# Layer 1 of a two-layer attention kernel: division by the softmax sums taken out of the groups, last blocks of two sets turned together, projection run in the drain

## The chip, the cores and the metric

The kernel runs on one core of one Trainium2 chip. The metric is the device time of one execution in microseconds; the median of several executions is compared. The program is unrolled: every loop below is written out into the instruction streams of the engines. TensorE (PE) multiplies and transposes into PSUM (eight banks of 128 partitions x 512 float32), VectorE (DVE), ScalarE (ACT) and GpSimd (POOL) work on elements, and SyncE (SP) issues the DMAs. Each engine takes its instructions in the order in which the program emits them and waits on semaphores for the others.

## The reference

Two layers over N = 4096 nodes with 512 features and 8 heads of 64, all in float32. Layer 0 is a graph attention layer with additive scores; layer 1, cut to what matters here, is

```python
h = jnp.maximum(_layernorm(x), 0.0)
keys, queries, values = (jnp.einsum('nj,hjk->hnk', h, W) for W in (Wks, Wqs, Wvs))
atts = jnp.einsum('hqk,hmk->hqm', queries, keys) / 64 ** 0.5
atts = atts - 1e16 * (1.0 - adj)[None, :, :]          # adj: [4096, 4096]
atts = jax.nn.softmax(atts, axis=-1)
x = x + jnp.einsum('hqm,hmk,hko->qo', atts, values, Wo)
```

## The kernel before

Layer 0 (lines 80 to 488), its last head pair together with the keys, queries and values of layer 1 (to line 780), then layer 1's attention (lines 791 to 1060) and at last the projection by `Wo` (lines 1063 to 1084). The change lies in the last two.

Layer 1 works on a pair of heads `c` (`HC` = 4 of them), then on groups of 128 query rows (`NG` = 32), then on sets of 32 rows (`GS` = 4 a group): 4 x 32 x 4 = 512 sets, one a slot `s` of the main loop (line 1021). A set holds 32 queries on 32 partitions for each of `NS` = 4 blocks of 1024 keys (`QK_`), so that one tile of 128 x 1024 holds 32 whole rows of scores of one head. The ring `t` keeps 12 sets (`RING`), each with two heads.

The order of the work is written by hand: a set passes through the slots with fixed delays. In slot `s`:

- `squares` (line 934, set s-4): DVE transposes 32 x 32 squares in place for columns 0 to 767 of both heads.
- `turned` (line 938, set s-4): PE transposes the last 256 columns (two 128 x 128 blocks for each of two heads) into one PSUM bank, tile `tr`; `taken` (line 947) copies them back to `t` on ACT.
- `smallest` (line 910, odd slots, sets s-3 and s-2): PE gathers the extremes of the four key blocks (`nmB`, a matmul with `bands`), DVE reduces them to `nm`.
- one step of `finish` (line 966) of the last group, see below.
- `scores` (line 871, set s): 32 matmuls of PE into four banks `sc`; `masked` (line 887): four DVE instructions add the penalty `a` and keep the extreme of the row.
- `taken`, then `exps` (line 924, set s-3): ACT takes the exponential in place and adds up the row (`G.sm`).
- `made_penalty` (line 862) for set s+1 where c = 0: Relu on ACT, then POOL makes the penalty from the adjacency; it is stored in `pen_d` and loaded from there for c > 0.
- `parted` (line 900, odd slots): POOL lays out the extremes for `smallest`.
- `weighted` (line 950, set s-8): 32 matmuls of PE with the values, accumulated over the group's four slots in one bank `o`.
- the loads for slot s+5 on SP.

`finish` divides and turns back. It copies `o` to `oT` on ACT, forms the rows' sums by eight-fold short matmuls with `band` (`den`, line 972), takes the reciprocal on DVE (`rden`); one slot later PE transposes `oT` back to rows (`back`, line 979), DVE multiplies (`att`, line 981), and SP stores 128 x 128 to `att_d`, which lies in rows of nodes. PSUM is full: four banks for `sc`, one for `tr`, two for `ms` (`nmB`, `den`, `back`), one for `o`.

After the loop the projection loads, for each of 32 row blocks, 128 rows of `x1_d` and of `att_d`, transposes the latter (`atr`, line 1075), copies it (`aT`), multiplies by `wot` (`oo`, line 1080), adds and stores.

Of the kernel before, what the change touches and what calls it, by code (L numbers as in the profile page):

```python
# [8 lines left out]
F32 = mybir.dt.float32  # L9
# [3 lines left out]
PSUM = bass.MemoryType.PSUM  # L13
DRAM = bass.MemoryType.DRAM

P = 128
# [7 lines left out]
def kernel(  # L24
# [14 lines left out]
    nc = tc.nc  # L39
    N, DM = x.shape  # L40
    H, D = src_proj.shape[1:]
    HD = H * D
    NB = N // P
    KC = DM // P
    HC = HD // P
# [6 lines left out]
    dram = ctx.enter_context(tc.tile_pool(name="dram", bufs=1, space=DRAM))  # L52

    ident = const.tile([P, P], F32, name="ident")
# [5 lines left out]
    SQ = 32  # L60
    NS = P // SQ
    band = const.tile([P, SQ], F32, name="band")
    nc.vector.tensor_reduce(band, ident.rearrange("p (a j) -> p j a", j=SQ), AX.X, ALU.add)
    bands = const.tile([P, P], F32, name="bands")
# [28 lines left out]
    PR = 2 * D  # L93
# [5 lines left out]
    with tc.tile_pool(name="a0k", bufs=1) as pk, tc.tile_pool(name="a0v", bufs=4) as pv, tc.tile_pool(  # L99
        name="a0a", bufs=3  # L100
# [72 lines left out]
        def turned(G, i):  # L173

            trs = []
            for b in range(MB):
                if b % 4 == 0:
                    tr = ptr.tile([P, TW], F32, name="tr")
                    trs.append(tr)
                for h in range(2):  # L180
                    nc.tensor.transpose(  # L181
                        tr[:, bass.ts(b % 4 * 2 + h, P)], G.t[h][:, bass.ts(i * MB + b, P)], ident
                    )
            return trs
# [231 lines left out]
        def step(n):  # L416
            return groups[n // 2], n % 2
# [83 lines left out]
    with tc.tile_pool(name="b0c", bufs=1) as pc, tc.tile_pool(name="b0a", bufs=4) as pa, tc.tile_pool(  # L501
# [114 lines left out]
        def squares(G, k):  # L616
            u = t[:, G.ring + k].rearrange("p h (n j) -> p h n j", j=SQ)
            nc.vector.transpose(u, u)  # L618
# [160 lines left out]
            while jobs:  # L779
                work()  # L780
    l0.close()
    att_d = dram.tile([N, HD], F32, name="att_d")
    pen_d = dram.tile([N // 32, P, N // 4], F32, name="pen_d")

# [5 lines left out]
    VC = 768  # L792
    NV = VC // SQ
    NT = (QK_ - VC) // P
    with tc.tile_pool(name="a1t", bufs=1) as pt, tc.tile_pool(name="a1k", bufs=4) as pkk, tc.tile_pool(
        name="a1v", bufs=GS
    ) as pv, tc.tile_pool(name="a1a", bufs=6) as pa, tc.tile_pool(name="a1q", bufs=2) as pq, tc.tile_pool(
        name="a1x", bufs=1
    ) as px, tc.tile_pool(name="a1s", bufs=6) as psb, tc.tile_pool(
        name="a1sc", bufs=4, space=PSUM  # L800
    ) as psc, tc.tile_pool(name="a1tr", bufs=1, space=PSUM) as ptr, tc.tile_pool(
        name="a1m", bufs=2, space=PSUM
    ) as pm, tc.tile_pool(name="a1o", bufs=1, space=PSUM) as po:
        t = pt.tile([P, RING, 2, QK_], F32, name="t")
        class Group:


# [115 lines left out]

        def exps(G, k):
            if k == 0:
                G.sm = psb.tile([P, GS, 2], F32, name="sm")
            for h in range(2):
                u = t[:, G.ring + k, h, :]
                nc.scalar.activation(  # L929
                    u, u, AF.Exp, bias=G.nm[k // 2][:, k % 2, h : h + 1], scale=-1.0,  # L930
                    accum_out=G.sm[:, k, h : h + 1],
                )

        def squares(G, k):
# [1 line left out]
            nc.vector.transpose(u, u)  # L936

        def turned(G, k):
            tr = ptr.tile([P, 512], F32, name="tr")
            for h in range(2):  # L940
                for m in range(NT):
                    nc.tensor.transpose(  # L942
                        tr[:, bass.ts(h * NT + m, P)], t[:, G.ring + k, h, bass.ds(VC + m * P, P)], ident
                    )
            return tr

        def taken(G, k, tr):
            nc.scalar.copy(t[:, G.ring + k, :, VC:], tr.rearrange("p (h x) -> p h x", h=2))  # L948

        def weighted(G, i):  # L950
            if i == 0:
# [12 lines left out]
                    )  # L964

        def finish(G):

            oT = px.tile([P, P], F32, name="oT")
            nc.scalar.copy(oT, G.o[:, :P])  # L969
            den = pm.tile([P, 512], F32, tag="ms", name="den")  # L970
            for k in range(GS):
                nc.tensor.matmul(  # L972
                    den[bass.ts(k, SQ), :2], lhsT=band, rhs=G.sm[:, k, :], start=True, stop=True
                )
            rden = psb.tile([P, 2], F32, name="rden")
            nc.vector.reciprocal(rden, den[:, :2])
            yield
            back = pm.tile([P, 512], F32, tag="ms", name="back")
            nc.tensor.transpose(back[:, :P], oT, ident)  # L979
            att = px.tile([P, 2, D], F32, name="att")  # L980
            nc.vector.tensor_mul(
                att, back[:, :P].rearrange("p (h d) -> p h d", d=D),
                rden.unsqueeze(2).to_broadcast([P, 2, D]),
            )
            nc.sync.dma_start(
                att_d[bass.ts(G.g, P), bass.ts(G.c, PR)], att.rearrange("p h d -> p (h d)")
            )

        groups = [Group(c, g) for c in range(HC) for g in range(NG)]
        total = len(groups) * GS  # L990
# [12 lines left out]
        with tc.manual_schedule():  # L1003
            pens = {}

            def prefetch(n):
                if n < total:
                    if n % (QG * GS) == 0:
                        load_queries(n // (QG * GS))
                    pens[n] = penalty(*step(n))  # L1010

            AHEAD = 5
            ending = iter(())
            load_keys(0)
            for n in range(AHEAD):
                prefetch(n)
            with_self(*step(0), pens[0])
            made_penalty(*step(0), pens[0])
            for i in range(GS):
                load_values(0, i)  # L1020
            for s in range(total + PROD + 3):
                if s + 1 < total:
                    with_self(*step(s + 1), pens[s + 1])
                if s < total:
                    keep_penalty(*step(s), pens[s])

                c, at = divmod(s + 4, SETS)
                if 0 < c < HC and at == 0:
                    load_keys(c)
                c, at = divmod(s - PROD - 1 + GS, SETS)  # L1030
                if 0 < c < HC and at < GS:
                    load_values(c, at)
                turn = 0 <= s - TURN < total
                if turn:
                    squares(*step(s - TURN))
                    tr = turned(*step(s - TURN))

                if s % 2 and 0 <= s - 3 < total:
                    G, k = step(s - 3)
                    smallest(G, k // 2)  # L1040
                next(ending, None)
                if s < total:
                    scs = scores(*step(s))
                    masked(*step(s), scs, pens.pop(s))
                if turn:
                    taken(*step(s - TURN), tr)
                if 0 <= s - EXPS < total:
                    exps(*step(s - EXPS))
                if s + 1 < total:
                    made_penalty(*step(s + 1), pens[s + 1])  # L1050
                if s % 2 and s < total:
                    G, k = step(s)
                    parted(G, k // 2)
                n = s - PROD
                if 0 <= n < total:
                    W, w = step(n)
                    weighted(W, w)
                    if w == GS - 1:
                        ending = finish(W)
                prefetch(s + AHEAD)  # L1060


    with tc.tile_pool(name="p3c", bufs=1) as pc, tc.tile_pool(name="p3", bufs=4) as pw, tc.tile_pool(
        name="p3t", bufs=3, space=PSUM
    ) as pst, tc.tile_pool(name="p3m", bufs=3, space=PSUM) as psm:
        wot = pc.tile([P, HC, DM], F32, name="wot")
        nc.scalar.dma_start(wot, wo.rearrange("h d o -> (h d) o").rearrange("(c p) o -> p c o", p=P))
        for rb in range(NB):
            xt = pw.tile([P, DM], F32, name="xt")
            nc.sync.dma_start(xt, x1_d[bass.ts(rb, P), :])  # L1070
            at = pw.tile([P, HD], F32, name="at")
            nc.sync.dma_start(at, att_d[bass.ts(rb, P), :])
            tr = pst.tile([P, 512], F32, name="atr")
            for c in range(HC):
                nc.tensor.transpose(tr[:, bass.ts(c, P)], at[:, bass.ts(c, P)], ident)
            aT = pw.tile([P, HD], F32, name="aT")
            nc.scalar.copy(aT, tr)  # L1077
            o = psm.tile([P, 512], F32, name="oo")
            for c in range(HC):
                nc.tensor.matmul(  # L1080
                    o, lhsT=aT[:, bass.ts(c, P)], rhs=wot[:, c, :], start=(c == 0), stop=(c == HC - 1)
                )
            nc.vector.tensor_add(xt, xt, o)
            nc.sync.dma_start(out[bass.ts(rb, P), :], xt)


# [26 lines left out]
```

## Time and profile before

| what | value |
|---|---|
| time, median of 3 runs | 5032.46 us (5031.23 to 5033.24) |
| profiled execution: its time, its span | 5033.3 us, 5031.5 us |
| PE, DVE, ACT, POOL busy, of the span | 95%, 90%, 78%, 7% |
| granted TensorE clock, mean | 0.978 |
| layer 1: first and last start of `sc` | 2542.8 and 4862.8 us |
| projection: first `atr`, last `oo` | 4893.6 and 5027.1 us |
| one `o` group of 32 matmuls, `sc` of 32, four `tr` | 1.97, 1.95, 0.66 us |

Times are from the start of the span. A PE matmul's duration reaches over the beginning of the next, so what an operation takes of PE is read from the starts of what follows. PEld is PE's loading of weights, which overlaps matmuls. In the listings a row gives the start, the duration, the engine, the line, the operation, the tiles written and read, and in brackets the engine's idle time before it with what ended it. "issue" is time in which the engine waited for nothing that the profile shows.

### The profile page before, as it was taken

What the parts mean: (1) busy time and instruction counts of PE and PEld (TensorE: products, weight loads), DVE (VectorE), ACT (ScalarE), POOL (GpSimd) and SP (SyncE); (2) the same over time, 40 slices, a digit from 0 to 9 for tenths busy, and PEclk for the clock granted to TensorE, in tenths of its full rate; (3) what the DMA queues carried; (4) which work ended last, traced back from release to release, by engine and by line L of the source; (5) the groups of instructions that cost most, each with busy time, mean ns of one, the idle gap of its engine ahead of it and who ended that gap; (6) DMA issues with size and microseconds to landing.
All of it is one profiled execution on the core that took longest, in us unless ns stands there. A gap on an engine that the chain in (4) does not pass through costs nothing.

```text
span 5031.5 us, 147684 instructions
## 1 busy us (share of the span) xinstructions
PE 4802.4 (95%) x62810; PEld 3552.2 (71%) x62810; DVE 4530.7 (90%) x8205; ACT 3929.0 (78%) x4581; POOL 362.1 (7%) x648
## 2 busy tenths in 40 slices
PE   6999999999999869999989999999999999999999
PEld 5888888888888757677746666666666666666654
DVE  4999999999999898888579999999999999999971
ACT  3999999999999898888568888666666666666651
POOL 1000000000000011111112222000000000000000
PEclk8999999999999979999999999999999999999999
DMA  6444454445444474444387777433353434444425
GB/s 217 152 163 146 163 194 163 147 161 195 163 147 161 129 167 134 141 140 138 98 240 240 237 239 246 145 124 126 126 160 122 127 127 143 141 127 127 127 98 176
DMA packets 339908, 794.35 MB, mean 158 GB/s; under 512 B 57520, under 2 KB 168368, under 8 KB 314160
## 3 DMA queue, kind: packets, MB, share of 16 engines
q1 hardware_dynamic: 338720, 783.86, 48.7%
q8 instruction: 493, 8.08, 0.7%
q14 instruction: 167, 1.37, 0.1%
q10 hardware_dynamic: 528, 1.05, 0.1%
HBM read 652.48 MB, written 132.25 MB: 156 GB/s over the span
## 4 chain that ended last, share of the span: by engine, by line
PE 46%; DMA 1%; ACT 1%; issue 1%; DVE 1%; SPq 0%; POOL 0%; ACTq 0%; DVEq 0%; POOLq 0%
PE o L959 18%; PE sc L878 18%; PE tr L942 6%; PE oo L1080 2%; DMA a<-in_adj_dram 1%; ACT t L929 1%; PE nmB L913 1%; PE den L972 0%; DVE t L936 0%; PE back L979 0%; SPq L852 0%; PE mp L697 0%; DVE t L894 0%; ACT aT L1077 0%; PE mpv L709 0%
## 5 line engine op out<-in xcount | busy, mean ns | idle before, releaser
L894 DVE CUSTOM_DVE_ANT_0 t<-sc,a 128x512 f32<-128x512 f32 x2048 | 1291.1, 686 | 78.2 <-issue 56.3
L929 ACT ACTIVATE t<-t,nm 128x1024 f32<-128x1024 f32 x1024 | 1168.4, 1143 | 167.6 <-DVE nm L918 167.6
L959 PEld LDWEIGHTS o<-t,v 128*64 128x64 f32 x16384 | 883.9, 137 | 423.2 <-issue 339.7
L878 PE MATMUL sc<-k,q 64*32 64x512 f32 x16384 | 1002.5, 597 | 8.9 <-DVE nm L894 8.9
L959 PE MATMUL o<-t,v 128*64 128x128 f32 x16384 | 1007.0, 276 | 0.2 <-ACT oT L969 0.2
L936 DVE STREAM_TRANSPOSE t<-t 128x1536 f32<-128x1536 f32 x512 | 908.1, 1774 | 8.9 <-ACT t L929 5.9
L158 DVE CUSTOM_DVE_ANT_0 t<-t,a 128x2048 f32<-128x2048 f32 x384 | 876.1, 2282 | 28.7 <-ACT t L147 23.6
L181 PE MATMUL tr<-ident,t 128*128 128x128 f32 x6144 | 781.7, 278 | 38.1 <-ACT pT L190 20.0
L181 PEld LDWEIGHTS tr<-ident,t 128*128 128x128 f32 x6144 | 665.4, 141 | 130.6 <-issue 65.5
L203 PE MATMUL o<-pT,v 128*64 128x128 f32 x12288 | 756.8, 276 | 0.8 <-DVE pT L192 0.8
L147 ACT ACTIVATE t<-tb,src 128x4096 f32<-128x4096 f32 x192 | 732.0, 3813 | 13.7 <-DMA tb<-trg_d 13.7
L168 ACT ACTIVATE t<-t,nm 128x4096 f32<-128x4096 f32 x192 | 731.7, 3811 | 6.9 <-DVE nm L163 6.6
L203 PEld LDWEIGHTS o<-pT,v 128*64 128x64 f32 x12288 | 664.1, 137 | 60.7 <-issue 46.9
L948 ACT COPY t<-tr 128x512 f32<-128x512 f32 x512 | 298.9, 584 | 480.2 <-PE tr L942 477.4
L192 DVE COPY pT<-tr 128x1024 f32<-128x1024 f32 x549 | 652.7, 1214 | 9.8 <-PE tr L181 9.8
L878 PEld LDWEIGHTS sc<-k,q 64*32 64x32 f32 x16384 | 251.0, 106 | 340.7 <-issue 298.5
L942 PE MATMUL tr<-ident,t 128*128 128x128 f32 x2048 | 342.6, 287 | 11.5 <-ACT t L929 9.5
L569 ACT ACTIVATE lk<-tb,srcb 128x1024 f32<-128x1024 f32 x256 | 282.3, 1113 | 83.5 <-DVE nm L579 76.4
L579 DVE CUSTOM_DVE_ANT_0 bt<-lk,ba 128x1024 f32<-128x1024 f32 x256 | 301.9, 1215 | 25.6 <-ACT e L703 12.7
L618 DVE STREAM_TRANSPOSE bt<-bt 128x2048 f32<-128x2048 f32 x128 | 295.1, 2306 | 29.0 <-ACT bt L611 29.0
L942 PEld LDWEIGHTS tr<-ident,t 128*128 128x128 f32 x2048 | 213.7, 140 | 111.3 <-issue 85.0
L611 ACT ACTIVATE bt<-bt,nm 128x1024 f32<-128x1024 f32 x256 | 290.3, 1135 | 0.4 <-DVE nm L600 0.3
(116 smaller groups left out, 3961.4 us busy)
## 6 DMA issues: line engine op xcount, KB each, us to landing
a<-in_adj_dram SPq DMA_DIRECT2D x192, 1024.0 KB
a<-pen_d SPq DMA_DIRECT2D x384, 512.0 KB
ba<-in_adj_dram SPq DMA_DIRECT2D x512, 128.0 KB
a<-in_adj_dram SPq DMA_DIRECT2D x512, 128.0 KB
pen_d<-a SPq DMA_DIRECT2D x128, 512.0 KB
h<-hT_d SPq DMA_DIRECT2D x96, 256.0 KB
qk_d<-e SPq DMA_DIRECT2D x64, 256.0 KB
x<-in_x_dram SPq DMA_DIRECT2D x8, 1024.0 KB
```

Source lines behind the costliest of these rows:

```text
L147: nc.scalar.activation(t, targets[G.c, h], AF.Prelu, bias=src[:, G.g, 2 * G.c + h : 2 * G.c + h + 1], alpha=SLOPE)
L158: nc.vector.tensor_tensor_reduce(out=t, in0=t, in1=rows_of_adj[G, f], scale=-1.0, scalar=FMAX, op0=ALU.add, op1=ALU.min, accum_out=nm[:, f ...
L168: nc.scalar.activation(G.t[h], G.t[h], AF.Exp, bias=G.nm[h][:, NCH : NCH + 1], scale=-1.0, accum_out=G.sm[:, h : h + 1],)
L181: nc.tensor.transpose(tr[:, bass.ts(b % 4 * 2 + h, P)], G.t[h][:, bass.ts(i * MB + b, P)], ident)
L192: nc.vector.tensor_copy(pT, tr)
L203: nc.tensor.matmul(G.o[h * D : (h + 1) * D, :P], lhsT=feats[G.c][i][:, b, bass.ts(h, D)], rhs=pT[:, bass.ts(b % 4 * 2 + h, P)], start=(mb ...
L878: nc.tensor.matmul(sc[h][bass.ts(a, SQ), :], lhsT=G.q[bass.ts(h, D), bass.ds(G.q0 + k * SQ, SQ)], rhs=keys[G.c][half][bass.ts(h, D), a, :] ...
L894: nc.vector.tensor_tensor_reduce(out=t[:, G.ring + k, h, cols], in0=scs[half][h], in1=a[:, cols], scale=1.0, scalar=FMAX, op0=ALU.add, op1 ...
L929: nc.scalar.activation(u, u, AF.Exp, bias=G.nm[k // 2][:, k % 2, h : h + 1], scale=-1.0, accum_out=G.sm[:, k, h : h + 1],)
L936: nc.vector.transpose(u, u)
L942: nc.tensor.transpose(tr[:, bass.ts(h * NT + m, P)], t[:, G.ring + k, h, bass.ds(VC + m * P, P)], ident)
L959: nc.tensor.matmul(G.o[bass.ts(h, D), :P], lhsT=v[:, b, bass.ts(h, D)], rhs=t[:, bass.ds(G.ring, GS), h, bass.ds(at, SQ)], start=(mb == 0) ...
```

## The change

- `finish` is one ACT copy of `o` to `oT` and one store, into an `att_d` that now lies as [head pair, 128 features, nodes]. It is emitted at the start of the slot after the group's last `weighted`.
- The sums of all rows are kept in a tile `sums`. Sixteen groups (a half of a head pair) are divided at once: `inverted` forms the sums by one matmul with `bands`, takes the reciprocal, turns it and stores it in `inv_d`; `scaled` loads four pieces of `att_d` of 512 columns with the reciprocals broadcast over the partitions, multiplies on POOL (on DVE for the last half) and stores them back. One step of this is taken in each slot.
- `turned` and `taken` run in odd slots alone, for the sets s-5 and s-4 together: eight transposes into two banks, one copy of 128 x 1024. The pool of `ms` falls from two banks to one.
- The projection needs no transposes, since `att_d` lies turned. Its loads come in chunks of two row blocks; `projected` runs from slot 513 on, one row block a slot, and the rest after the loop. Before the ninth chunk's load all that is left of the last division is emitted.

```diff
@@ -779,8 +779,12 @@
             while jobs:
                 work()
     l0.close()
-    att_d = dram.tile([N, HD], F32, name="att_d")
+    att_d = dram.tile([HC, P, N], F32, name="att_d")
+    inv_d = dram.tile([HC, 2, N], F32, name="inv_d")
     pen_d = dram.tile([N // 32, P, N // 4], F32, name="pen_d")
@@ -792,16 +796,19 @@
     VC = 768
     NV = VC // SQ
     NT = (QK_ - VC) // P
+    SG = NG // 2
     with tc.tile_pool(name="a1t", bufs=1) as pt, tc.tile_pool(name="a1k", bufs=4) as pkk, tc.tile_pool(
         name="a1v", bufs=GS
     ) as pv, tc.tile_pool(name="a1a", bufs=6) as pa, tc.tile_pool(name="a1q", bufs=2) as pq, tc.tile_pool(
-        name="a1x", bufs=1
-    ) as px, tc.tile_pool(name="a1s", bufs=6) as psb, tc.tile_pool(
+        name="a1x", bufs=2
+    ) as px, tc.tile_pool(name="a1s", bufs=6) as psb, tc.tile_pool(name="a1z", bufs=2) as pz, tc.tile_pool(name="a1at", bufs=3) as pat, tc.tile_pool(
         name="a1sc", bufs=4, space=PSUM
     ) as psc, tc.tile_pool(name="a1tr", bufs=1, space=PSUM) as ptr, tc.tile_pool(
-        name="a1m", bufs=2, space=PSUM
+        name="a1m", bufs=1, space=PSUM
     ) as pm, tc.tile_pool(name="a1o", bufs=1, space=PSUM) as po:
         t = pt.tile([P, RING, 2, QK_], F32, name="t")
+        sums = pt.tile([P, HC, 2, 2, SG, GS], F32, name="sums")
         class Group:
@@ -923,12 +930,12 @@
         def exps(G, k):
             if k == 0:
-                G.sm = psb.tile([P, GS, 2], F32, name="sm")
+                G.sm = sums[:, G.c, G.g // SG, :, G.g % SG, :]
             for h in range(2):
                 u = t[:, G.ring + k, h, :]
                 nc.scalar.activation(
                     u, u, AF.Exp, bias=G.nm[k // 2][:, k % 2, h : h + 1], scale=-1.0,
-                    accum_out=G.sm[:, k, h : h + 1],
+                    accum_out=G.sm[:, h, k : k + 1],
                 )
         def squares(G, k):
@@ -936,16 +943,19 @@
             nc.vector.transpose(u, u)
         def turned(G, k):
-            tr = ptr.tile([P, 512], F32, name="tr")
-            for h in range(2):
-                for m in range(NT):
-                    nc.tensor.transpose(
-                        tr[:, bass.ts(h * NT + m, P)], t[:, G.ring + k, h, bass.ds(VC + m * P, P)], ident
-                    )
+            tr = ptr.tile([P, 2, 2, NT * P], F32, name="tr")
+            for j in range(2):
+                for h in range(2):
+                    for m in range(NT):
+                        nc.tensor.transpose(
+                            tr[:, j, h, bass.ts(m, P)],
+                            t[:, G.ring + k - 1 + j, h, bass.ds(VC + m * P, P)], ident,
+                        )
             return tr
         def taken(G, k, tr):
-            nc.scalar.copy(t[:, G.ring + k, :, VC:], tr.rearrange("p (h x) -> p h x", h=2))
+            nc.scalar.copy(t[:, bass.ds(G.ring + k - 1, 2), :, VC:], tr)
         def weighted(G, i):
             if i == 0:
@@ -964,27 +974,88 @@
                     )
         def finish(G):
             oT = px.tile([P, P], F32, name="oT")
             nc.scalar.copy(oT, G.o[:, :P])
-            den = pm.tile([P, 512], F32, tag="ms", name="den")
-            for k in range(GS):
+            nc.sync.dma_start(att_d[G.c, :, bass.ts(G.g, P)], oT)
+        def inverted(c, half):
+            tot = pm.tile([P, 512], F32, tag="ms", name="tot")
+            nc.tensor.matmul(
+                tot[:, : 2 * SG * GS], lhsT=bands,
+                rhs=sums[:, c, half].rearrange("p h g k -> p (h g k)"), start=True, stop=True,
+            )
+            inv = px.tile([P, P], F32, tag="oT", name="inv")
+            nc.vector.reciprocal(inv[:SQ], tot[:SQ, : 2 * SG * GS])
+            yield
+            invT = pm.tile([P, 512], F32, tag="ms", name="invT")
+            nc.tensor.transpose(invT[:, :SQ], inv[:SQ], ident[:SQ, :SQ])
+            rows = px.tile([P, SQ], F32, name="rows")
+            nc.scalar.copy(rows, invT[:, :SQ])
+            for h in range(2):
+                nc.sync.dma_start(
+                    inv_d[c, h, bass.ts(half, SG * P)].rearrange("(q i) -> q i", i=SQ), rows[bass.ts(h, D)]
+                )
+            yield
+        def scaled(c, half):
+            last = (c, half) == (HC - 1, 1)
+            zs = []
+            for i in range(4):
+                cols = bass.ts(half * 4 + i, 4 * P)
+                z = pz.tile([P, 2, 4 * P], F32, tag="z", name="z")
+                nc.sync.dma_start(z[:, 0], att_d[c, :, cols])
+                for h in range(2):
+                    nc.sync.dma_start(z[bass.ts(h, D), 1], inv_d[c, h, cols].partition_broadcast(D))
+                yield
+                zs.append((cols, z))
+                if i % 2 == 0:
+                    continue
+                yield
+                for cols, z in zs:
+                    (nc.vector if last else nc.gpsimd).tensor_mul(z[:, 0], z[:, 0], z[:, 1])
+                yield
+                for cols, z in zs:
+                    nc.sync.dma_start(att_d[c, :, cols], z[:, 0])
+                zs = []
+        def divided(c, half):
+            yield from inverted(c, half)
+            yield from scaled(c, half)
+        ZR = 2
+        chunks = []
+        def load_chunk():
+            i = len(chunks)
+            if i >= NG // 2 // ZR:
+                for d in divisions:
+                    for _ in d:
+                        pass
+                divisions.clear()
+            if i < NB // ZR:
+                at = pat.tile([P, HC, ZR * P], F32, name="at")
+                nc.sync.dma_start(at, att_d[:, :, bass.ts(i, ZR * P)].rearrange("c p n -> p c n"))
+                xt = pa.tile([P, ZR, DM], F32, tag="a", name="xt")
+                nc.sync.dma_start(xt, x1_d[bass.ts(i, ZR * P), :].rearrange("(r p) d -> p r d", p=P))
+                chunks.append((at, xt))
+        def projected(j):
+            if j >= NB:
+                return
+            i, r = divmod(j, ZR)
+            at, xt = chunks[i]
+            o = psc.tile([P, HF], F32, tag="sc", name="oo")
+            for c in range(HC):
                 nc.tensor.matmul(
-                    den[bass.ts(k, SQ), :2], lhsT=band, rhs=G.sm[:, k, :], start=True, stop=True
-                )
-            rden = psb.tile([P, 2], F32, name="rden")
-            nc.vector.reciprocal(rden, den[:, :2])
-            yield
-            back = pm.tile([P, 512], F32, tag="ms", name="back")
-            nc.tensor.transpose(back[:, :P], oT, ident)
-            att = px.tile([P, 2, D], F32, name="att")
-            nc.vector.tensor_mul(
-                att, back[:, :P].rearrange("p (h d) -> p h d", d=D),
-                rden.unsqueeze(2).to_broadcast([P, 2, D]),
-            )
-            nc.sync.dma_start(
-                att_d[bass.ts(G.g, P), bass.ts(G.c, PR)], att.rearrange("p h d -> p (h d)")
-            )
+                    o, lhsT=at[:, c, bass.ts(r, P)], rhs=wot[:, c, :], start=(c == 0), stop=(c == HC - 1)
+                )
+            nc.vector.tensor_add(xt[:, r], xt[:, r], o)
+            if r == ZR - 1:
+                nc.sync.dma_start(out[bass.ts(i, ZR * P), :].rearrange("(r p) d -> p r d", p=P), xt)
+                load_chunk()
         groups = [Group(c, g) for c in range(HC) for g in range(NG)]
         total = len(groups) * GS
@@ -1010,7 +1081,8 @@
                     pens[n] = penalty(*step(n))
             AHEAD = 5
-            ending = iter(())
+            rb = 0
+            divisions = []
             load_keys(0)
             for n in range(AHEAD):
                 prefetch(n)
@@ -1033,12 +1105,19 @@
                 turn = 0 <= s - TURN < total
                 if turn:
                     squares(*step(s - TURN))
+                turn = turn and (s - TURN) % 2
+                if turn:
                     tr = turned(*step(s - TURN))
                 if s % 2 and 0 <= s - 3 < total:
                     G, k = step(s - 3)
                     smallest(G, k // 2)
-                next(ending, None)
+                n = s - PROD
+                if 0 < n <= total and n % GS == 0:
+                    finish(groups[n // GS - 1])
+                if s > total:
+                    projected(rb)
+                    rb += 1
                 if s < total:
                     scs = scores(*step(s))
                     masked(*step(s), scs, pens.pop(s))
@@ -1051,37 +1130,23 @@
                 if s % 2 and s < total:
                     G, k = step(s)
                     parted(G, k // 2)
-                n = s - PROD
                 if 0 <= n < total:
                     W, w = step(n)
                     weighted(W, w)
-                    if w == GS - 1:
-                        ending = finish(W)
+                if n > 1 and n % (SG * GS) == 1:
+                    divisions.append(divided(*divmod(n // (SG * GS) - 1, 2)))
+                for d in divisions[:1]:
+                    if next(d, d) is d:
+                        divisions.pop(0)
+                if s == (HC - 1) * SETS + SETS // 2:
+                    wot = pkk.tile([P, HC, DM], F32, tag="k", name="wot")
+                    nc.sync.dma_start(wot, wo.rearrange("h d o -> (h d) o").rearrange("(c p) o -> p c o", p=P))
+                if s > total - AHEAD and len(chunks) < 3:
+                    load_chunk()
                 prefetch(s + AHEAD)
-    with tc.tile_pool(name="p3c", bufs=1) as pc, tc.tile_pool(name="p3", bufs=4) as pw, tc.tile_pool(
-        name="p3t", bufs=3, space=PSUM
-    ) as pst, tc.tile_pool(name="p3m", bufs=3, space=PSUM) as psm:
-        wot = pc.tile([P, HC, DM], F32, name="wot")
-        nc.scalar.dma_start(wot, wo.rearrange("h d o -> (h d) o").rearrange("(c p) o -> p c o", p=P))
-        for rb in range(NB):
-            xt = pw.tile([P, DM], F32, name="xt")
-            nc.sync.dma_start(xt, x1_d[bass.ts(rb, P), :])
-            at = pw.tile([P, HD], F32, name="at")
-            nc.sync.dma_start(at, att_d[bass.ts(rb, P), :])
-            tr = pst.tile([P, 512], F32, name="atr")
-            for c in range(HC):
-                nc.tensor.transpose(tr[:, bass.ts(c, P)], at[:, bass.ts(c, P)], ident)
-            aT = pw.tile([P, HD], F32, name="aT")
-            nc.scalar.copy(aT, tr)
-            o = psm.tile([P, 512], F32, name="oo")
-            for c in range(HC):
-                nc.tensor.matmul(
-                    o, lhsT=aT[:, bass.ts(c, P)], rhs=wot[:, c, :], start=(c == 0), stop=(c == HC - 1)
-                )
-            nc.vector.tensor_add(xt, xt, o)
-            nc.sync.dma_start(out[bass.ts(rb, P), :], xt)
+            for j in range(rb, NB):
+                projected(j)
 # ---- launch: one core; inputs and outputs as the reference has them ----
```

## The prediction

> **What bounds the kernel now.** I read the page, then the busy times by stage, then the order of time inside a few slots, then the waits, then the chain. The stages first (columns: stretch, length, busy time of PE, PEld, DVE, ACT, POOL, granted clock, DMA share, GB/s): layer 1's first head pair, its last one, the final projection.
>
> ```profile
> core 0: us, PE busy (x) PEld busy (x) DVE busy (x) ACT busy (x) POOL busy (x), PEclk, DMA share, GB/s
> 2560.00:3100.00 540.00, 525.94 (x8169) 321.75 (x8155) 525.36 (x1280) 447.76 (x729) 134.65 (x176) 0.99 0.77 244
> 4300.00:4850.00 550.00, 550.00 (x8692) 344.00 (x8688) 526.91 (x1219) 362.68 (x642) 14.59 (x61) 1.00 0.41 128
> 4900.00:5020.00 120.00, 118.98 (x360) 57.98 (x359) 20.30 (x30) 16.11 (x30) 0.00 (x0) 1.00 0.57 184
> ```
>
> In three of four head pairs PE never stops; DVE idles 23 of 550 us. In the first pair (where the penalty is made) PE idles 14 us too. The projection is PE alone. So PE's order of time in the last pair, four slots less a little (start, us, what):
>
> ```profile
> 4301.87 1.95 PE L878 MATMUL sc<-k,q 64*32 64x512 f32 x32
> 4303.75 1.97 PE L959 MATMUL o<-t,v 128*64 128x128 f32 x32
> 4305.65 0.66 PE L942 MATMUL tr<-ident,t 128*128 128x128 f32 x4
> 4306.23 0.24 PE L972 MATMUL den<-sm,band 128*32 128x2 f32 x8
> 4306.41 1.95 PE L878 MATMUL sc<-k,q 64*32 64x512 f32 x32
> 4308.29 1.97 PE L959 MATMUL o<-t,v 128*64 128x128 f32 x32
> 4310.19 0.66 PE L942 MATMUL tr<-ident,t 128*128 128x128 f32 x4
> 4310.68 0.31 PE L913 MATMUL nmB<-parts,bands 128*128 128x32 f32 x2
> 4310.82 0.31 PE L979 MATMUL back<-ident,oT 128*128 128x128 f32 x1
> 4311.06 1.95 PE L878 MATMUL sc<-k,q 64*32 64x512 f32 x32
> 4312.94 1.97 PE L959 MATMUL o<-t,v 128*64 128x128 f32 x32
> 4314.83 0.66 PE L942 MATMUL tr<-ident,t 128*128 128x128 f32 x4
> 4315.42 1.95 PE L878 MATMUL sc<-k,q 64*32 64x512 f32 x32
> ```
>
> Durations overlap, so costs are differences of starts: sc 1.88, o 1.90 (32 weight loads take 1.73, the rest is a gap of 0.17 before tr). A slot from sc to sc is 4.54 with den, 4.65 with nmB and back, 4.36 with neither, and 4.50 with nmB alone (4315.42 to 4319.93): 18.05 a group of four.
>
> The first pair has another loop. There the mask of an even slot comes right after the penalty that POOL made for it:
>
> ```profile
> 2812.72 1.04 POOL L865 TENSOR_SCALAR a<-a 128x1024 f32<-128x1024 f32 x1 [4.25 <-ACT a L864]
> ...
> 2813.87 0.65 DVE L894 CUSTOM_DVE_ANT_0 t<-sc,a 128x512 f32<-128x512 f32 x1
> ```
>
> And the tail, from the chain: PE falls idle 6.14 us until the attention rows come back, then takes 8.08 us per two row blocks, of which 6.9 are the 16 projection matmuls (0.43 each) and the rest transposes.
>
> ```profile
> 4887.35 6.14 DMA at<-att_d
> ...
> 4902.80 7.13 PE oo L1080 x16
> ```
>
> **The change part by part.** The steady part is c=1 to 3: 96 groups.
>
> Den and back leave PE: 4.54-4.36 = 0.18 and 4.65-4.50 = 0.15, so 0.33 a group. On DVE rden (0.13) and att (0.20 between starts) leave too; there they free an engine that is not the bound.
>
> Turning by twos. An even slot loses tr and the gap after it, 0.59 (4314.83 to 4315.42). An odd slot gets eight transposes for four: layer 0 issues 16 in 1.73, so four more cost 0.43. The unknown is o followed directly by sc, which the trace never shows. Its tiles go from 128*64 to 64*32, and every change of tile shape that it does show (o to tr, tr to sc, tr to den) carries a 0.17 gap in the weight loads. The Trainium skill, "TensorEngine Tiling (Array Packing)", Key Properties, says that a change of tiling mode drains the engine. That speaks against the step: only one drain of the two goes. Bounds: 0 (the pair saves 0.33, the sum falls by 33 more) to 0.34, rows and columns both changing (it saves nothing). I take 0.17, the nearest row, which is inside o's 1.90. A pair of slots goes from 8.86 to 2x(1.88+1.90) + 0.72 + 0.44 = 8.72 (0.72: tr with nmB to sc now, 4319.20 to 4319.93). The group: 18.05 - 0.33 - 2x0.14 = 17.44; times 96, -58.6 us.
>
> Does anything else bind before 8.72? The slots become uneven (PE 3.78 and 4.94), so I laid out one pair from sc of the even slot at 0: o 1.88, tr 3.78, nmB 4.71, sc 4.94, o 6.82. DVE: four masks are 2.45, the 32x32 turning 1.70, nm 0.07 more; 8.37 a pair, so it waits 0.35 for the odd sc (mask 1.27 after sc, as in 4306.41 to 4307.68). ACT: the merged copy starts 1.17 after tr, at 4.95, and by layer 0's copy of the same 128x1024 takes 1.10, to 6.05; nm is ready at 5.97, so exps run 6.05 to 8.43 and the turning on DVE, due at 8.66, is served with 0.2 to spare. The next exps end at 10.8 (11.6 behind an oT copy), the next eight transposes need them at 12.5. ACT's loop through nm, exps, turning, mask, turning is 8.52. PE stays the bound, by 0.2. The copy oT now opens an even slot and ends by 0.4, its o bank is wanted at 1.88. One bank less for ms costs nothing: its reader nm is done two slots before.
>
> First pair, c=0: the loop nm, two exps, Relu, POOL's penalty, mask is 4.67 (2799.98 to 2804.65 in order of time), mask back to nm 4.45 (2813.87 to 2818.32): 9.12 a pair of slots, and the stage runs at just that. Nothing of it is touched; DVE alone would give 0.33 a group, 10 us. I take -1, between 0 and -10.
>
> Divisions, eight halves, seven inside the loop. PE: tot and invT, each like back (0.15 to 0.31) plus a drain: 0.5. DVE: a reciprocal of 128 columns (att's 0.28 is the nearest row) that waits for tot about 0.5; half is in DVE's slack. ACT: rows, 0.2. +4 in all, between 1 and 10. POOL: 28 products of 128x512; from 0.24 us at 32 columns (parts) and 0.46 at 128 (L241), 1.3 each as an estimate, up to 2.1 (L676's 128x512). Two stand ahead of parts, which nmB wants 4.8 us after its masks, and ahead of the next penalty in c=0, which has 4 us: hidden. "SBUF — State Buffer", Terms, has a lock between DVE and GpSimd under which the loser fully blocks: by it 28x1.3 = 36 us of DVE waiting, of which perhaps 20 would show. The trace speaks otherwise for these operations: in c=0, POOL lies under the turning in every slot, and that takes 1775 ns against 1773 later. I take 0. SP: att_d writes stay 128 (behind oT instead of att), and a half adds 12 loads, 6 writes, about 0.35 to 0.45 of issue each. SP stands at the z stores until POOL is done, with the penalty loads behind it; those are five slots (22 us) ahead. Cover enough; if gone, each us late is a us of PE. The extra 24 MB meet a DMA share of 0.41.
>
> The tail, from the last sc (4861.42) to the end, is 170.1 now. After: sc 1.9, nine o 17.1, a wait for exps 1.0, two turns 2.4, 32 projections of 8x0.43 = 110.1, tot and invT 0.9: 133.4. Ten projections fill the draining slots; the aT transposes and copies are gone. But the last half can be divided only after o's last group: the flush after projection 11 runs add 0.7, six issues 2.6, landing 3, two products 1.4, store 2.9, again six issues, landing and products 7, stores 0.8, chunk load 6 (the 6.14 above as top): some 24.5 us, while PE has four projections, 13.8. A stall of 11, then a cold clock (the first eight projection matmuls took 6.29 against 3.7 after the idle 6 us, granted clock 0.52): 2.6. With 3.8 for the last add and store: 151. That is -19, between -33 (no stall) and 0 (30 us of stall).
>
> Sum: -58.6 - 1 + 4 - 19 = -74.6. The profiled execution took 5033.3 (span 5031.5 and 1.8 around it), 0.8 over the median: 4958.7, and against the median 4958.
>
> **The rivals.** (1) o to sc drains twice, or the uneven slots cost what the pairing saves: 0.28x96 = 27 back, 4985. For it: rows and columns of the tile change at once. Against: tr to den also went at 0.17. (2) No drain: pair 8.55, just above ACT's 8.52: 4925. Against: every shape change shown has its gap. (3) The flush stalls PE for 30 us, as each step waits for the whole of att_d: 4977. For it: SP is in order and the loads and stores alternate. (4) Slower: the z loads land late, POOL waits at the product with parts behind it, and nmB, sc and all else stand. The loads have two slots, then parts another two, some 20 us; each us beyond costs one, in 14 rounds (seven halves of two). It eats 74 us and turns the sign from 25 us of landing on. Against: loads land within 6 us in the chain, with DMA at full load. (5) The change does what it says but its gain in c=0 is DVE's 10: 4949.
>
> **How the numbers follow.** My forecast 0.55 (4945 to 4972), (1) 0.14, (2) 0.11, (3) 0.10, (4) with other losses 0.05, (5) 0.05. The range 4926 to 4994 leaves out (4), half of (2) and a combination of (1) with (3). 0.2% (10 us) is what a measurement of this kernel tells from no change. Faster 0.93, same 0.02, slower 0.05.
>
> **What would show it.** Stretches in c=1 to 3: PE busy throughout, 17.4 us a group, odd slots 4.9, even 3.8; the weight loads of sc with a 0.17 gap after o. The copy of tr 256 times at 1.10. DVE idle 0.3 to 0.4 a pair before the odd mask. c=0 unchanged at 9.1 a pair. In the tail an idle PE of about 11 us near projection 16, then 3.44 a row block. The forecast is wrong if PE idles in c=1 to 3 before tr (ACT late) or before nmB (POOL late), or if sc starts over 0.2 after o's last load.

## The result and the profile after

The changed kernel takes 4986.92 us (median of 4 runs, 4984.33 to 4987.83) against 5032.85 us before: ratio 0.9907, 95% interval 0.9889 to 0.9924. It is faster by 46 us; 74.6 were forecast. The profiled execution took 4984.33 us with a span of 4982.5.

Where the time went is read from the starts of the first mask (`masked`) of slots 0, 128 and 511, in the profiled execution of each kernel:

| stage | before | after | difference | forecast |
|---|---|---|---|---|
| up to slot 0 (code not changed) | 2544.1 | 2538.9 | -5.1 | 0 |
| first head pair, c=0 | 590.3 | 622.7 | +32.4 | -1 |
| c=1 to 3, to slot 511 | 1728.3 | 1672.1 | -56.2 | -54.6 (with the divisions) |
| slot 511 to the end | 168.9 | 148.8 | -20.1 | -19 |

The first row is drift: in the other profiles below it lies anywhere from 2539.9 to 2547.8. Two stages came out as worked out; the first head pair went the other way. The busy times by stage (the columns as before) give no hint of it, except that PE is busier in c=0, although the stage is longer:

```profile
2560.00:3100.00 540.00, 532.42 (x7549) 313.30 (x7551) 526.88 (x1169) 418.79 (x634) 132.61 (x170) 0.99 0.74 237
4300.00:4820.00 520.00, 520.00 (x8236) 331.19 (x8228) 502.62 (x1134) 339.96 (x569) 24.34 (x68) 1.00 0.44 147
4850.00:4970.00 120.00, 110.54 (x409) 53.08 (x406) 23.20 (x33) 1.73 (x4) 0.00 (x0) 0.96 0.61 203
```

Before, PE was busy 525.94 of 540 us in the same stretch of c=0 with 8169 matmuls; now 532.42 with 7549. A busy time that rises while the work falls is matmuls that wait inside their own duration. Here they are those of `sc`: 3552 of them take 268.4 us, where 3728 took 229.2, and PE's idle time before them is ended by DVE's masks (9.1 us, 6.0 before), which free their banks.

PE's order of time in the last head pair after, from sc of an even slot on:

```profile
4303.41 1.95 PE L885 MATMUL sc<-k,q 64*32 64x512 f32 x32
4305.29 1.97 PE L969 MATMUL o<-t,v 128*64 128x128 f32 x32
4307.19 1.09 PE L951 MATMUL tr<-ident,t 128*128 128x128 f32 x8
4308.12 0.31 PE L920 MATMUL nmB<-parts,bands 128*128 128x32 f32 x2
4308.35 1.95 PE L885 MATMUL sc<-k,q 64*32 64x512 f32 x32
4310.23 1.97 PE L969 MATMUL o<-t,v 128*64 128x128 f32 x32
4312.13 1.95 PE L885 MATMUL sc<-k,q 64*32 64x512 f32 x32
```

An odd and an even slot last 8.72 (4303.41 to 4312.13), and o followed by sc takes 1.90 (4310.23 to 4312.13).

Now the first head pair, where a pair of slots grew from 9.2 to 9.7. Before, in a slot with `nmB`, DVE's maximum for the self-edges (`with_self`, line 860) was over just before POOL made the penalty (line 865):

```profile
2807.21 0.18 DVE L860 TENSOR_TENSOR a<-a,ident 32x32 f32<-32x32 f32 x1
...
2807.43 1.05 POOL L865 TENSOR_SCALAR a<-a 128x1024 f32<-128x1024 f32 x1 [2.61 <-ACT a L864]
```

In other slots it was closer still. In 22 of the 128 the maximum started ahead of POOL by 0.013 us or less, as here:

```profile
2724.72 0.18 DVE L860 TENSOR_TENSOR a<-a,ident 32x32 f32<-32x32 f32 x1
2724.73 1.08 POOL L865 TENSOR_SCALAR a<-a 128x1024 f32<-128x1024 f32 x1 [2.45 <-ACT a L864]
```

After, POOL is first, and the same maximum (now line 867) takes 0.81:

```profile
2912.87 1.04 POOL L872 TENSOR_SCALAR a<-a 128x1024 f32<-128x1024 f32 x1 [2.12 <-ACT a L871]
2913.03 0.08 DVE L901 DVE_READ_ACCUMULATOR2_ANT nm<- 128x1 f32 x1
2913.14 0.81 DVE L867 TENSOR_TENSOR a<-a,ident 32x32 f32<-32x32 f32 x1
2913.98 1.78 DVE L943 STREAM_TRANSPOSE t<-t 128x1536 f32<-128x1536 f32 x1
```

It ends at 2913.95, 0.04 after POOL does (2913.91). The turning, the next nm and both masks are late by 0.6. In the instruction list 59 of the 128 maxima are so, all but one of every second one from the ninth on. All 128 together take 56.7 us, and 24.2 before. The 32.5 us more are the 32.4 of the table. Nobody is listed as waiting: the time is inside the instruction, so the waits of DVE say nothing. Only the duration of the one instruction does (count, then min/median/max in ns, before and after):

```profile
L860 DVE TENSOR_TENSOR a<-a,ident x128: 169/183/1016, 2536.8 to 3123.9; 32x32 f32<-32x32 f32 x128
```

```profile
L867 DVE TENSOR_TENSOR a<-a,ident x128: 170/189/926, 2531.6 to 3151.2; 32x32 f32<-32x32 f32 x128
```

Even this row hides it: the median still falls on the short half. The one long case before (1.016) was the same collision: there POOL had started 0.06 us ahead of the maximum.

In the tail PE stops once more, for the ninth chunk, as the chain shows:

```profile
4914.97 5.34 DMA at<-att_d
4920.31 0.14 issue
4920.45 57.56 PE oo L1052 x128
```

PE has been idle for 9.46 us when projection 16 starts, and the last 128 matmuls take 57.56 instead of 55.0 (0.43 each); the granted clock was 0.56 from 4920 to 4926 and 1.00 after.

### The profile page after: what moved, and what is told of

It reads as the page before. It is cut to its first block, busy times and chain, and to the rows that moved or that the text cites. A ratio compares the mean times of both kernels' runs of the same rounds, so it can differ in the third digit from the quotient of the medians.

```text
span 4982.5 us, 144240 instructions
## 1 busy us (share of the span) xinstructions
PE 4757.9 (95%) x61554; PEld 3525.6 (71%) x61554; DVE 4522.0 (91%) x7961; ACT 3856.4 (77%) x4301; POOL 396.4 (8%) x676
## 5 line engine op out<-in xcount | busy, mean ns | idle before, releaser
L885 PE MATMUL sc<-k,q 64*32 64x512 f32 x16384 | 1059.3, 598 | 11.9 <-DVE nm L901 11.8
L943 DVE STREAM_TRANSPOSE t<-t 128x1536 f32<-128x1536 f32 x512 | 907.6, 1773 | 4.1 <-ACT t L936 1.1
L181 PE MATMUL tr<-ident,t 128*128 128x128 f32 x6144 | 781.6, 278 | 38.2 <-ACT pT L190 20.1
L181 PEld LDWEIGHTS tr<-ident,t 128*128 128x128 f32 x6144 | 665.3, 141 | 130.7 <-issue 65.4
L958 ACT COPY t<-tr 128x1024 f32<-128x1024 f32 x256 | 259.0, 1012 | 515.1 <-PE tr L951 503.8
L885 PEld LDWEIGHTS sc<-k,q 64*32 64x32 f32 x16384 | 263.2, 106 | 402.0 <-issue 234.1
L626 PE MATMUL bo<-bt,bv 128*64 128x128 f32 x4096 | 284.2, 298 | 6.2 <-ACT boT L635 4.9
L951 PE MATMUL tr<-ident,t 128*128 128x128 f32 x2048 | 280.6, 280 | 2.0 <-ACT t L936 2.0
```

The costliest lines, as they stand in the source:

```text
L181: nc.tensor.transpose(tr[:, bass.ts(b % 4 * 2 + h, P)], G.t[h][:, bass.ts(i * MB + b, P)], ident)
L885: nc.tensor.matmul(sc[h][bass.ts(a, SQ), :], lhsT=G.q[bass.ts(h, D), bass.ds(G.q0 + k * SQ, SQ)], rhs=keys[G.c][half][bass.ts(h, D), a, :] ...
L951: nc.tensor.transpose(tr[:, j, h, bass.ts(m, P)], t[:, G.ring + k - 1 + j, h, bass.ds(VC + m * P, P)], ident,)
```

## The experiments

All start from the changed kernel unless said otherwise. Stages as in the table above; "max" is DVE's busy time in the 128 self-edge operations (where two overlap, the time counts once). m1 and m2 ran twice, the others four times or more.

| kernel | median us | c=0 | c=1 to 3 | tail | max |
|---|---|---|---|---|---|
| before | 5032.85 | 590.3 | 1728.3 | 168.9 | 24.2 |
| changed | 4986.92 | 622.7 | 1672.1 | 148.8 | 56.7 |
| e2, maximum moved | 4947.83 | 579.9 | 1672.3 | 149.1 | 19.6 |
| e3, filler on ACT | 4954.94 | 588.9 | 1672.1 | 148.8 | 23.5 |
| e4, no pairing | 4989.95 | 592.4 | 1702.0 | 149.7 | 24.9 |
| m1, one input | 4957.4 | 589.7 | 1672.1 | 148.7 | 25.8 |
| m2, constant operand | 4989.53 | 622.0 | 1672.1 | 149.3 | 55.9 |
| t1, flush early | 4978.98 | 621.4 | 1672.1 | 140.2 | 56.7 |
| b2, both mends | 4938.88 | 578.3 | 1672.3 | 142.2 | 18.8 |
| u1, before with maximum moved | 5030.48 | 586.1 | 1728.3 | 169.1 | 18.6 |

**e2: the maximum at another place.**

```diff
...
-                if s + 1 < total:
-                    with_self(*step(s + 1), pens[s + 1])
...
                     smallest(G, k // 2)
+                if s % 2:
+                    for j in (s + 2, s + 3):
+                        if j < total:
+                            with_self(*step(j), pens[j])
```

> The changed kernel, with the self-edge maximum (L867, 32x32, both inputs in SBUF) of two sets moved from the head of each slot to odd slots, just before the masks, where POOL has nothing to do. Theory A (DVE's maximum is held up by POOL's penalty, 0.65 to 0.92 us in every odd slot instead of 0.18): all 128 take about 0.18, the first head pair falls from 621 us to 580 to 592 (pair of slots 9.0), the rest is as it was, 4950 to 4958 in all. Theory B (the first head pair is slower because the merged copy of 1.01 us stands before exps on ACT, or because the division's loads crowd SP): it stays at 615 to 625, 4987 in all.

4947.83 us, ratio to before 0.9829 (0.9813 to 0.9845). The first head pair fell by 43 us, a pair of slots is 8.82, and the other stages stayed. The list shows the maximum short again, but for one that still met POOL:

```profile
L867 DVE TENSOR_TENSOR a<-a,ident x128: 156/180/935, 2531.8 to 3110.3; 32x32 f32<-32x32 f32 x128
```

Theory A holds (the time came out 2 us under what it said); neither the merged copy nor the division's loads, both still there, cost what was lost. The place has a price of its own: the second maximum needs its adjacency two slots sooner, and during the first division DVE stood before it twice, for 2.2 and 3.4 us (pairs of slots of 11.1 and 13.0). That it stood for the adjacency is inferred; the profile lists these waits as "issue".

**e3: work added to ACT.**

```diff
...
                     taken(*step(s - TURN), tr)
+                elif s < SETS:
+                    nc.scalar.copy(idle, bands.unsqueeze(1).to_broadcast([P, 4, P]))
```

> The changed kernel, with an added ACT copy of 128x512 into a scratch tile before exps in the slots of the first head pair that have no copy of tr any more; it is pure extra work. Theory A (the copy's leaving the even slots lets Relu, and with it POOL's penalty, come 0.6 us earlier, onto DVE's maximum): the penalty moves behind the maximum again, which takes 0.18, and the first head pair falls from 621 us to 585 to 598; 4952 to 4965 in all. Theory B (ACT has too much to do in the first head pair): it gets slower, 4987 to 5010.

4954.94 us (0.9843; 0.9828 to 0.9857): with 66 useless copies of 0.60 us each the kernel is 32 us faster than without. The order of time shows why: the filler (line 1128), and in the next slot Relu (872), the maximum (868) and the penalty (873):

```profile
2912.76 0.61 ACT L1128 COPY idle<-bands 128x512 f32<-128x512 f32 x1
...
2915.56 1.04 ACT L872 ACTIVATE a<-a 128x1024 f32<-128x1024 f32 x1
2916.43 0.18 DVE L868 TENSOR_TENSOR a<-a,ident 32x32 f32<-32x32 f32 x1
...
2916.68 1.05 POOL L873 TENSOR_SCALAR a<-a 128x1024 f32<-128x1024 f32 x1 [2.64 <-ACT a L872]
```

Against the end of DVE's masks, Relu ends and POOL starts some 0.5 later than in the changed kernel, POOL starts after the maximum, and the maximum is short again. So it is the copy's leaving of the even slots that moved POOL onto DVE.

**e4: the pairing undone.**

```diff
...
-                turn = turn and (s - TURN) % 2
...
-            tr = ptr.tile([P, 2, 2, NT * P], F32, name="tr")
...
+            tr = ptr.tile([P, 512], F32, name="tr")
...
-            nc.scalar.copy(t[:, bass.ds(G.ring + k - 1, 2), :, VC:], tr)
+            nc.scalar.copy(t[:, G.ring + k, :, VC:], tr.rearrange("p (h x) -> p h x", h=2))
```

> The changed kernel, with the turning by PE of the last 256 columns undone: four transposes and a copy of 128x512 in every slot, as before the change; all else kept (no den, no back, divisions, projection in the drain). Theory A: without the pairing the maximum is not held up; the first head pair takes 575 to 590, the other three rise from 8.72 to 8.86 a pair of slots (27 us more), 4972 to 4984 in all: the pairing as it was made is worth nothing. Theory B (divisions or their loads slow the first head pair): it stays near 620 and the time rises to about 5014.

4989.95 us, ratio 0.9913 (0.9898 to 0.9928), not to be told from the changed kernel's. The stages tell it: the other pairs rise by 29.9 us (8.87 a pair of slots), and the first falls by 30.3. Theory A on the mechanism; the forecast band was missed by 6 us, of which c=0 (592 and not up to 590; three maxima still met POOL) and the other pairs (29.9 and not 27) make up 5. The pairing, as it was made, gave nothing in all.

**m1 and m2: which DVE operation is held up.** At the maximum's place another operation on the same block.

```diff
-                nc.vector.tensor_max(diag, diag, ident[bass.ts(b, SQ), bass.ts(b, SQ)])
+                nc.vector.transpose(diag, diag)                        # m1
+                nc.vector.tensor_scalar(diag, diag, 0.0, None, ALU.max)  # m2
```

> The changed kernel; at the place of the self-edge maximum DVE transposes the same 32x32 block in place instead (one input in SBUF; the self-edges are left out and the block is turned, the output is not the reference's). If what is held up by POOL's penalty is an operation with two inputs in SBUF: every instruction takes its own short time (under 0.25 us), the first head pair falls to 575 to 595. If POOL's instruction holds up any operation of DVE: every second one still takes 0.6 to 0.9 and the stage stays near 620.

> The changed kernel; at the place of the self-edge maximum DVE takes the maximum of the same 32x32 block with the constant 0 instead (tensor_scalar, one input in SBUF, which the skill's page on SBUF counts among the operations that can still enter a two-port mode; the self-edges are left out). If the two-port form is used and held up by the same lock: every second one takes 0.6 to 0.9 us and the first head pair stays near 620. If only two inputs count: under 0.25 us each, 575 to 595.

In m1 the transpose starts under POOL in 59 slots and is as short there as elsewhere; in the list its maximum is 209 ns:

```profile
2915.68 1.05 POOL L872 TENSOR_SCALAR a<-a 128x1024 f32<-128x1024 f32 x1 [2.11 <-ACT a L871]
2915.97 0.20 DVE L867 STREAM_TRANSPOSE a<-a 32x32 f32<-32x32 f32 x1
```

```profile
L867 DVE STREAM_TRANSPOSE a<-a x128: 189/202/209, 2535.9 to 3122.6; 32x32 f32<-32x32 f32 x128
```

In m2 an operation with a constant, one input in SBUF, is held up just like the maximum:

```profile
L867 DVE TENSOR_SCALAR a<-a x128: 158/178/923, 2537.0 to 3155.9; 32x32 f32<-32x32 f32 x128
```

So neither "any operation" nor "two inputs" is the whole rule. The two operations that were held up are just those that the Trainium skill, "SBUF — State Buffer", Who interferes with whom, names: with two inputs in SBUF, or of a kind that can enter a two-port mode; whoever starts first holds the pair of ports that DVE and POOL share for its whole instruction. The trace agrees where POOL came first: in all 59 slots the operation ended 0.03 to 0.04 us after POOL, and a transpose, which the page does not name, goes free. Where the maximum came first, by at most 0.013 us (22 slots of the kernel before), it took 0.18 as it does alone, and POOL took 1.08 to 1.10 instead of 1.04 to 1.07. That is at most 0.05 longer, though the maximum ended 0.17 to 0.18 after POOL's start, so for this order the trace does not show that the whole overlap is waited for.

**t1: the flush.** After the loop, ahead of projection 10:

```diff
...
+            for d in divisions:
+                for _ in d:
+                    pass
+            divisions.clear()
             for j in range(rb, NB):
                 projected(j)
```

and in `scaled`, for the last half, four buffers, all loads first, the broadcast ones from ACT.

> The changed kernel, with the rest of the last division emitted right after the loop (before projection 10 instead of after projection 11), its four pieces loaded at once (four z buffers, the broadcast loads issued by ACT). If the 9.5 us in which PE is idle before projection 16 and the slow matmuls after it (2.5 us) come from the flush: the idle time is under 1 us and the time falls by 10 to 12, to 4975 to 4977. If the idle time comes from the chunk loads themselves: it stays, within 3 us of 4987.

4978.98 us (0.9893; 0.9878 to 0.9907); by medians not clear of the changed kernel, by its stage 8.6 us shorter. PE's idle time fell from 9.46 to 3.13, not below 1, and the time missed what was expected by 2 us. What is late next:

```profile
4906.84 13.57 PE L1064 MATMUL oo<-wot,at 128*128 128x512 f32 x31 [3.13 <-DVE xt L1067]
```

The sums of projections 10 to 13 stand on DVE behind the four products, and the projections have four banks to write to.

**b2: both mends**, the products put back behind projection 11, the loads left early.

> The changed kernel with both mends: the self-edge maximum moved as in e2_max_moved, and of the last division the four pieces loaded right after the loop (four z buffers, broadcast loads issued by ACT), while products and stores stay where the flush was, after projection 11, so that the sums of projections 10 and 11 no longer stand behind them. If the two losses are independent: e2_max_moved's 4948 less t1_flush_early's 8, less the 3 us that PE still idled there and a part of the slow start after it: 4934 to 4940. If they share a cause, it stays above 4943.

4938.88 us, ratio 0.981 (0.9797 to 0.9824), 95 us under the kernel before and 48 under the changed one: the fastest here, and the two losses are independent. PE still waits 3.46 us in the tail, now for the chunk itself:

```profile
4877.03 56.87 PE L1065 MATMUL oo<-wot,at 128*128 128x512 f32 x128 [3.46 <-DMA at<-att_d]
```

So the tail did not become shorter than t1's (142.2 against 140.2); this half of the mend was worth nothing.

**u1: the kernel before, with the maximum moved as in e2.**

> The kernel before, with only the self-edge maximum moved as in e2_max_moved. There the maximum was never held up (0.18), so theory A gives this move little: in the first head pair the pairs of slots go from 9.2 to between 8.9 and 9.2, 5013 to 5033 in all, and nothing changes in the other three. If e2_max_moved's gain of 39 us came from the move itself and not from the end of a collision, this kernel gains as much: about 4994.

5030.48 us (0.9992; 0.9986 to 0.9999): 3.5 us, 4.2 in the stage. In the kernel before the move is worth next to nothing, so of its 39 us in e2 some 35 are the end of a collision that the change had made. e3, which moves nothing of DVE's, says the same with 33.8 in the stage.

## Why the prediction was right or wrong

The time lies in the range and the sign was right, but the forecast was 29 us too low, outside the 4945 to 4972 that was held most likely. That the range held it is luck: its upper part was there for rivals (1) and (3), and what filled it was a loss that no step and no rival named. By its steps:

- **Den, back and pairing on PE: right.** 17.44 a group were forecast for c=1 to 3, two pairs of 8.72 were measured. The unknown, o followed by sc, takes the 0.17 of a drain: 1.90 from start to start. e4 gives the pairing 29.9 us there (27 forecast). The other 26.3 (1728.3 less 1702.0) are den and back, 0.31 a group (18.05 less two pairs of 8.87; 0.33 forecast) or 29.8, less 3.5 for the divisions. One reading was too wide: not every change of tile shape carries the gap. In the weight loads before, den to sc shows 0.02 and nmB to sc 0.04; o to sc, which counted, has its 0.17.
- **No other bound before 8.72: right**, and close: the copy of `tr` took 1.01 and not 1.10.
- **Divisions: +4 forecast.** By the starts of sc, two pairs in each of c=1 to 3 are 9.31 instead of 8.72, 0.59 each (0.5 forecast), 3.5 in all six. The reciprocal was mis-sized, 0.94 instead of 0.28, and it didn't matter. The POOL products took 1.29 each (1.3) and were hidden.
- **The tail: right.** From the last sc to the end 150.0 (4832.54 to 4982.5; 151 forecast), 9.5 us of stall at projection 16 (11), 2.5 of a slow start (2.6).
- **The first head pair: wrong, and more than the whole error.** It came out 33.4 above its forecast; the drift before slot 0 (5.1) and the two other stages (1.6 and 1.1) hide a part of that. The step said of its loop "Nothing of it is touched". The loop's own parts were not, and its value stands: with the collision away (e3) the stage takes 588.9, 1.4 less than before. What the step left out is that the copy left ACT's even slots. Relu, and POOL behind it, came some 0.5 earlier and met DVE's maximum. That maximum was not in my list of DVE's work for c=0, since 0.18 us seemed too little to matter. Held up, it cost 32.4 us. (Its reading of the stage was a little off too: the pairs before alternate between 9.12 and 9.22.)
- **The rule was at hand and weighed at the wrong place.** I took the lock between DVE and GpSimd for the new products on POOL and found the turning unharmed under POOL (1775 ns against 1773). That was right for the turning, as m1 confirms for its kind. I then said "for these operations" and did not go through DVE's other operations in the stage, of which one has both inputs in SBUF.
- **The rivals.** The time is that of rival (1), 4985, by accident: its mechanism, a second drain, is refuted by 1.90 and 8.72. (2), no drain and a pair of 8.55, falls by the same 1.90 and 8.72. (3) to (5) did not come.

One more step lies in c=0: a pair of slots grows from 8.91 to 9.15 after fifteen pairs in e3, e4 and m1 (from 9.0 to 9.2 before, from 9.6 to 9.7 after), and not where the maximum was moved (e2, b2, u1). The traces place it at set 32, the first whose 32x32 block lies on partitions 32 to 63 and no longer on 0 to 31. In e3 the maximum starts with the masks' last accumulator row up to set 31 (0.00 us) and 0.11 after it from set 32 on, and the turning starts 0.10 and then 0.21 after the maximum. The same step stands in before, after, e4, m1 and m2. That the partitions are the cause, and not something else that begins with set 32, was not tried; nor does this say why the moved maximum is spared.

## What to carry to other kernels

An engine that is relieved of work runs earlier, and what it triggers moves with it: ask for each operation moved not only what is late next, but what comes early now and onto what. Where two engines share a resource, list every operation of both in the stage, down to the shortest, and where each starts against the other; a gap of 0.04 us between two instructions, let alone 0.01, is luck, not order. Such a loss shows in no wait: look for instructions of one shape whose durations fall into two groups, in the single rows and not in the mean or the median.

## What the runs showed of the hardware

A 32x32 operation of DVE took 0.63 to 0.93 us instead of 0.18 when POOL's 128x1024 tensor_scalar was already under way, and ended 0.03 to 0.04 after it; a tensor_scalar with a constant was held up as a maximum of two tiles was (0.63 to 0.92 in 59 of 128), a transpose not at all (0.20). I had not expected that an operation with one input would be. POOL itself took 1.04 to 1.07 in those slots and without; only where the maximum had started just ahead of it was it a little longer (1.08 to 1.10).

From the first block on partitions 32 to 63 on, such an operation started 0.11 us after the DVE row before it instead of with it, and the next started 0.11 later still (0.21 instead of 0.10).
